# Heads of a two-layer graph network: projections step before the tails in each round

## The chip, the cores and the metric

The kernel runs on one core of one Trainium2 chip. The metric is the device time of one execution in microseconds (us). The engines are TensorE (PE, with its weight loads shown as PEld), VectorE (DVE), ScalarE (ACT), GpSimd (POOL) and SyncE (SP, which issues DMAs here).

## The reference

Two layers, each a graph convolution followed by a feed-forward block, over 3327 nodes of 256 features in fp32. The change touches only the last block, a causal attention with 4 heads and 4 queries per head. Cut to what it computes:

```python
sx = jnp.einsum('bsh,ndh->bnsd', x, hl_w) + hl_b[None, :, None, :]
pad = sx == 0
q = jnp.einsum('bnsd,neod->bneso', sx, wq)
k = jnp.einsum('bnsd,nod->bnso', sx, wk)
v = jnp.einsum('bnsd,nod->bnso', sx, wv)
scores = jnp.einsum('bnesd,bntd->bnest', q, k) * d ** 0.5 + causal
att = jax.nn.softmax(scores, axis=-1)
qkv = jnp.where(pad[:, :, None], 0.0, jnp.einsum('bnest,bntd->bnesd', att, v))
gs = jax.nn.softmax(gate of qkv, axis=-1)
mixed = jnp.einsum('bnsed,bnse->bnsd', ..., gs)
hn = layernorm(mixed + resid, ln_g, ln_b)
hx = relu(fx @ fc1_w.T + fc1_b) @ fc2_w.T + fc2_b     # masked where fx == 0
hx = layernorm(hx + fx, fnorm_g, fnorm_b)
fg = jax.nn.softmax(fout @ fgate_w.T, axis=-1)
return fout * fg (per head)
```

## The kernel before, in words

The nodes are padded to 26 tiles of 128 rows. The two graph layers and the experts come first; the function `heads` runs last, from about 975 us to the end, and is the only one that the change touches.

In `heads`, tile t of queries needs keys and values of tiles 0 to t. A unit is a tile and a head (104 units). The keys of a unit are cut into t // 4 + 1 chunks of at most 512, so there are 392 chunks, and the main loop (line 1422) makes one round for each. A round does, in the order in which the code issues it:

- `drain_to`: the scores of a later chunk are copied from PSUM to SBUF by DVE, with their maxima (`drain`, `sc<-pqk` in the profile). Where none are filled, `fill_next` first issues the matmuls that make them (`fill`, `pqk<-kt,qt`).
- `attend`: the weighted sum of the values on PE (`po<-sc,vr`).
- `turn`: the next chunk's weights are transposed in 32 by 32 blocks by DVE, the stream transposes `sc<-sc`.
- `values`: DMAs for a later chunk, issued by SP (`vr<-vs`).
- `weigh`: exponentials on ACT (`sc<-sc,anmax`), some here and the rest at the round's end.
- `back`: for a unit that ended in the round before, four matmuls with two outputs (`ptO`) and two copies by ACT (`qkv`, `glp`).
- `over`: for a unit that ends in this round, a copy `ot` (by ACT, then a multiply by POOL; for tiles below 5 one multiply by DVE).
- `run(tails)` and `run(preps)`, lines 1438 and 1439: each generator in the list makes one step. These two lines are what the change is about. From tile 8 on they are left out in a round that follows the end of a unit.
- the rest of `weigh`, and `fill_next` if no filled chunk is left.

A prep is the generator `prepare` (line 907), the projections of the next tile. Its nine steps are: a DMA for the row tile (`xres`); mean and variance by DVE (`pst`, `pmv`, `prs`); three POOL operations that make the normalised rows `xn`; their transpose on PE, copied out as `xt`; the projection `psxt` on PE, two ACT copies `sxt`, and the ACT pair Sign and Square into `nz`; four DMAs for `sxd` and the values `pv`, copied to `v`; the keys `pk`, copied to `kt`, and four DMAs that write `vs`; the queries `pq`, copied to `qt`; a transpose back, copied to `sx`. A prep starts in `begin` (line 1376), when the first scores of the tile before are filled. If it isn't finished when its own tile's first scores are due, `begin` runs its remaining steps at once, one after another, without the tails. In tiles 1 to 4 that is most of the prep.

A tail is the generator `tail` (line 1193), the part of a tile after its attention, in 21 steps: a small softmax over the gates (DVE, ACT `gss`, then POOL); POOL's weighted sum into `fx`; a layer norm (`norm4`, line 1169: a DVE sum `l1ns`, four ACT squares `sq`, then seven POOL operations); a transpose copied out as `fxt` and two Sign and Square pairs into `nzf`; the first matmul `ph`, copied out by ACT as `h`; a POOL multiply; the second matmul `ph`, copied out as `fo`, and three POOL operations; a second layer norm (`l2ns`, `sq`, POOL); a transpose copied out as `fot`, and a DMA for `xend`; a gate matmul `pfg`, read by DVE (`fgm`, `fgs`); a softmax; two POOL operations and the store. A tail takes longer than a tile in the early tiles, so up to four or five are in the list there; from about tile 16 one or two.

What sets the order: the class `InOrder` (line 50) chains every instruction of an engine to the one issued before it on that engine. So each engine runs in the order of the program text, and a step that stands second in a round waits behind the first one's instructions on that engine. Semaphores between engines are put in by the framework from the data dependencies and the reuse of buffers.

Buffers that matter: the pool `ps` (line 866) has four PSUM banks under one tag, for everything except `po`: the four score tiles of a chunk, `ptO`, and all outputs of preps and tails. They rotate in the order of the program text, so a new tile waits until the one allocated four before it has been read. The choice between ACT and DVE for a copy out of PSUM is made in `empty` (line 877) from running counters of both engines' work.

## Time and profile before

| what | value |
|---|---|
| time, median of 3 runs (lowest to highest) | 2971.8 us (2970.73 to 2976.79) |
| the profiled execution | 2971.83 us |
| its span, first to last instruction | 2970.1 us |
| mean granted TensorE clock | 0.973 |
| PE busy, 975 us to the end, by stretches of 50 to 200 us | 81 to 96% |
| DVE busy from 2000 to 2900 us | 97% |

The span is the time between the first and the last instruction on the core. Engine names stand first in a row of the profile; `a<-b` reads "a is written from b". A bracket such as `[4.80 <-POOL xn L61]` says that the engine was idle for 4.80 us before the instruction and that POOL's operation on `xn` ended it. All instructions of `heads` carry line 61, the line of the helper that chains them, so tiles, and not lines, tell them apart.

### The profile page before, as it was taken

Reading aid. Unit: us, or ns where it says so; the run is one execution under the profiler, and the core shown is the slowest. Engines: PE = TensorE matmul, PEld = TensorE weight load, DVE = VectorE, ACT = ScalarE, POOL = GpSimd, SP = SyncE. Lnnn points to the kernel's source line nnn. Section 1 sums busy time; section 2 is a strip of 40 time slices with the busy share of each in tenths; the row PEclk is TensorE's granted clock in tenths of the full one; section 3 lists DMA queues with packets and bytes.
Section 4 is the critical chain, followed back from the end, with each engine's and each line's share of the span. In section 5 each row is a group of like instructions: output and inputs, shape, how many; then the busy total and the mean of one; then the engine's idle time right before and its main releaser. Section 6 shows DMA issues by size and latency. Waiting matters only on the chain. (4 is left out here: it accounts for less than half of the span.)

```text
span 2970.1 us, 125328 instructions
## 1 busy us (share of the span) xinstructions
PE 2662.9 (90%) x53422; PEld 1966.3 (66%) x53422; DVE 2398.0 (81%) x5619; ACT 1813.9 (61%) x5128; POOL 973.8 (33%) x1448
## 2 busy tenths in 40 slices
PE   7999988879889788899999999999989999999996
PEld 6878887657668666566666666666666666656664
DVE  5102643689999577789999999999999999999997
ACT  6410135555555457677777776777777677676674
POOL 6441635622231146544433332322222222122121
PEclk9999999999999789999999999999999999999997
DMA  9994568648775222333333443443433433343432
GB/s 377 355 321 135 185 220 276 226 159 285 243 251 169 56 77 77 104 100 106 114 107 104 116 115 106 115 114 112 122 112 113 117 114 114 111 118 110 117 109 77
DMA packets 258188, 449.70 MB, mean 151 GB/s; under 512 B 58816, under 2 KB 156608, under 8 KB 257504
## 3 DMA queue, kind: packets, MB, share of 16 engines
q1 hardware_dynamic: 245536, 417.50, 45.6%
q0 software_dynamic: 6576, 18.02, 1.7%
q8 instruction: 421, 6.90, 1.0%
q10 hardware_dynamic: 5520, 6.18, 0.7%
q14 instruction: 135, 1.11, 0.1%
HBM read 393.37 MB, written 25.88 MB: 141 GB/s over the span
## 5 line engine op out<-in xcount | busy, mean ns | idle before, releaser
L61 ACT ACTIVATE sc<-sc,anmax 128x512 f32<-128x512 f32 (+3 forms) x1568 | 1040.4, 668 | 109.6 <-DVE anmax L61 109.4
L61 PEld LDWEIGHTS po<-sc,vr 32*64 32x64 f32 x43728 | 662.8, 131 | 395.2 <-DVE sc L61 234.0
L61 PE MATMUL po<-sc,vr 32*64 32x128 f32 x43728 | 765.2, 275 | 117.7 <-DVE sc L61 72.3
L61 DVE STREAM_TRANSPOSE sc<-sc 128x2048 f32<-128x2048 f32 (+3 forms) x392 | 816.2, 2082 | 24.2 <-ACT sc L61 23.9
L61 PE MATMUL pqk<-kt,qt 64*128 64x512 f32 (+3 forms) x3136 | 776.2, 579 | 24.5 <-ACT qt L61 4.8
L61 DVE TENSOR_SCALAR_CACHE_REDUCE sc<-pqk 128x512 f32<-128x512 f32 (+2 forms) x1152 | 655.5, 623 | 76.7 <-PE pqk L61 74.7
L61 PEld LDWEIGHTS pqk<-kt,qt 64*128 64x128 f32 x3136 | 319.2, 187 | 247.0 <-issue 102.5
L61 PE MATMUL acc<-wh,p 128*128 128x259 f32 x1352 | 310.0, 387 | 34.5 <-DVE p L61 34.4
L61 PEld LDWEIGHTS acc<-wh,p 128*128 128x128 f32 x1352 | 254.1, 190 | 92.7 <-DVE p L61 52.2
L61 PE MATMUL acc<-y,pan 128*128 128x256 f32 x1352 | 303.5, 385 | 12.2 <-DMA pan<-in_adjt_dram 10.5
L61 POOL TENSOR_TENSOR ot<-ot,sxd 128x512 f32<-128x512 f32 x83 | 105.7, 1273 | 601.1 <-ACT ot L61 588.2
L61 ACT ACTIVATION_READ_ACCUMULATOR sc<-sc,anmax 128x1 f32 x1568 | 299.4, 191 | 0.0
L61 PEld LDWEIGHTS acc<-y,pan 128*128 128x128 f32 x1352 | 257.8, 192 | 53.0 <-issue 17.5
L61 DVE CUSTOM_DVE_ANT_0 sc<-pqk,mask 128x512 f32<-128x512 f32 (+3 forms) x416 | 242.1, 636 | 38.4 <-PE pqk L61 38.0
L61 ACT ACTIVATE u<-u,d 128x512 f32<-128x512 f32 (+1 forms) x182 | 125.2, 688 | 159.4 <-DVE u L61 159.3
L61 DVE SCALAR_TENSOR_TENSOR u<-bc,d 128x512 f32<-128x512 f32 (+1 forms) x182 | 136.4, 750 | 0.1
L61 DVE SCALAR_TENSOR_TENSOR p<-pan,u 128x512 f32<-128x512 f32 (+1 forms) x182 | 126.9, 697 | 10.2 <-PE acc L61 6.1
L61 ACT COPY qkv<-ptO 128x256 f32<-128x256 f32 x104 | 38.5, 370 | 153.3 <-PE ptO L61 153.0
L61 ACT ACTIVATE junk<-ar 128x1664 bf16<-128x1664 f32 x52 | 82.7, 1591 | 65.9 <-DMA ar<-in_adj_dram 64.8
L61 PE MATMUL ptO<-igw,ot 128*128 128x68 f32 x832 | 117.2, 284 | 5.5 <-issue 2.3
L61 PEld LDWEIGHTS ptO<-igw,ot 128*128 128x128 f32 x832 | 102.4, 193 | 24.1 <-issue 17.5
L61 DVE CUSTOM_DVE_ANT_0 sg<-sg,dst 128x1664 bf16<-128x1664 bf16 (+2 forms) x56 | 99.9, 1791 | 1.2 <-ACT dst L61 1.0
(336 smaller groups left out, 2976.6 us busy)
## 6 DMA issues: line engine op xcount, KB each, us to landing
vr<-vs SPq DMA_DIRECT2D x976, 128.0 KB
ar<-in_adj_dram SPq DMA_DIRECT2D x104, 832.0 KB
vr<-vs SPq DMA_DIRECT2D x544, 96.0 KB
pan<-in_adjt_dram SPq DMA_DIRECT2D x156, 256.0 KB
pan<-in_adjt_dram SPq DMA_DIRECT2D x26, 1024.0 KB
pan<-in_adjt_dram SPq DMA_DIRECT2D x20, 832.0 KB
w1e<-w SPq DMA_DIRECT2D x59, 256.0 KB
took<-places SPq DMA_DIRECT2D x59, 129.0 KB
```

The lines of the kernel that those rows point to most:

```text
L61: made = make(*args, **kw)
```

## The change

In each round of the main loop that steps both lists, `run(preps)` is called before `run(tails)`. Nothing else is changed.

```diff
                 if not ended or u["t"] < 8:
+                    run(preps)
                     run(tails)
-                    run(preps)
                 ended = last
```

## The prediction

> **What bounds the kernel now.** First the page's busy line, then the same busy times in stretches, to see where the heads stage (from about 975 us) has room.

> ```profile
> PE 2662.9 (90%) x53422; PEld 1966.3 (66%) x53422; DVE 2398.0 (81%) x5619; ACT 1813.9 (61%) x5128; POOL 973.8 (33%) x1448
> ```
> ```profile
> 1250.00:1300.00 50.00, 45.07 (x1119) 32.13 (x1124) 40.36 (x102) 32.32 (x103) 24.28 (x34) 0.93 0.31 90
> ...
> 2200.00:2400.00 200.00, 184.24 (x5492) 125.98 (x5478) 195.36 (x444) 142.37 (x440) 47.80 (x67) 1.00 0.40 114
> ```

> Columns: stretch, length, busy PE, PEld, DVE, ACT, POOL, clock, DMA. The averages hide two regimes. Late, DVE is busy 195.36 of 200: an order can win only from the last 2 to 3%. At 1250 to 1300 nothing is full (PE 90%, DVE 81%): waits in chains set the pace. So I read PE's waits from 975 to 1500, then the rounds behind the longest.

> ```profile
> PE pt L61 <- POOL xn L61: 20.3, 6, 4.9
> ```
> ```profile
> 1199.88 0.23 POOL L61 TENSOR_SCALAR l2ns<-l2ns 128x4 f32<-128x4 f32 x1
> ...
> 1203.64 0.72 POOL L61 TENSOR_TENSOR fo<-fo,fnb 128x256 f32<-128x256 f32 x1
> ...
> 1204.32 0.56 POOL L61 TENSOR_TENSOR prs<-prs,nhalf 128x1 f32<-128x1 f32 x1
> ...
> 1206.20 0.69 PE L61 MATMUL pt<-ident,xn 128*128 128x128 f32 x2 [4.80 <-POOL xn L61]
> ```
> ```profile
> 1208.50 0.56 DVE L61 TENSOR_SCALAR_CACHE_REDUCE sc<-pqk 128x384 f32<-128x384 f32 x1 [3.01 <-PE pqk L61]
> ```

> This is tile 6. POOL works through a tail's second layer norm (l2ns to fnb); only then come the projection's three operations (prs, xn, xn). PE stands 4.80 us at the transpose of xn with the next scores behind it, and DVE then idles 3.01 us.

> [...] the scores at 1206.82 start after the late transpose. [...] Granted after the wait of 3.85 us in tile 7:

> ```profile
> 1258.00:1265.00 7.00, 7.00 (x127) 4.17 (x127) 4.37 (x9) 4.62 (x14) 0.00 (x0) 0.58 0.01 2
> ```

> Its eight score matmuls took 3.79 us (1258.13 to 1261.92); at 1638 four of the same shape took 1.03, so 2.06 for eight. [...]

> **The change part by part.** No instruction is added or removed. In each round that has both, every engine gets the projection's step before the tails'. Engine choice in `empty` stays: added up along the loop, the counters' margin from tile 2 on, where tails exist, is at least 1.5 towards ACT, and no swapped copy reaches that.

> (a) xn first on POOL, with gains in four rounds (waits 1.92, 4.80, 3.85, 1.41 in tiles 5 to 8; the other two of the six, at 978 and 1002, have no tail beside them). Tile 6: POOL is free at 1199.8 (end of ot), prs and xn need 1.83 (1204.32 to 1206.15), so xn is there at 1201.7 and PE waits 0.5 instead of 4.80. ACT: xt at 1202.8, the tail's fxt and nzf 1.16 (1201.54 to 1202.70), so the exponentials start at 1203.9, not 1207.20: 3.3 earlier; they last 3.9, and PE's values are then done, so ACT's 0.59 idle before ot goes too. DVE finishes the round's softmax at 1205.49 and goes on at once. In the following round the last copy out of PSUM is now h, about 3.85 after ot begins (ot 0.57, sxt 0.72, nz 0.85, fot 0.37, nzf 0.88, h 0.46): 1211.7, with a score pair (0.9) and its reduction (0.69) 1213.3, where 1216.93 was. Gain 3.6. Tile 7 alike: exponentials from 1255.5, ot at 1259.8 (1264.99 before, held by matmuls at the low clock), end at 1265.3 instead of 1270.23. Gain 4.8. In tiles 5 and 8 DVE had work through PE's wait; ACT alone gains. 0.3 each. Sum 9.0. The tail's norm ends 1.8 later, at 1206.2; the transpose that reads it follows no sooner than 1208.6 even with PE early, so the delay has cover of about 2.4; without it, it would cost the 1.8.

> (b) Key copies before the squares. Tiles 13 to 15:

> ```profile
> 1640.18 0.35 ACT L61 ACTIVATE sq<-fo,l2ns 128x64 f32<-128x64 f32 x1
> ...
> 1640.53 0.62 ACT L61 COPY kt<-pk 128x256 f32<-128x256 f32 x2
> ```
> ```profile
> 1640.93 1.13 PE L61 MATMUL pqk<-kt,qt 64*128 64x512 f32 x4 [1.25 <-ACT kt L61]
> ```

> Four squares (1638.76 to 1640.62) stand before kt, whose banks the scores need. PE waits 1.25, 1.24, 1.75; DVE behind it 1.07, 0.69, 0.46. Gain 2.2.

> (c) The gate's bank. A tail's pfg is read by DVE after a 2.3 us transpose; four banks rotate, so its place decides which score waits:

> ```profile
> 1968.66 0.61 PE L61 MATMUL pfg<-fgw,fot 128*128 128x4 f32 x4
> 1969.20 1.16 PE L61 MATMUL pq<-sxt,wq 64*128 64x128 f32 x16
> ...
> 1971.83 1.52 PE L61 MATMUL pqk<-kt,qt 64*128 64x384 f32 x6 [0.82 <-DVE gsm L61]
> ```

> Last in the order, it holds only the last score tile. Beside pq (tiles 17 to 20): 0.75, 0.75, 0.25, 0.25, from DVE's later waits there, up to 0.87; 2.0. Beside psxt (tiles 20 to 23, PE waits 0.72 to 0.75): a half of the stalled pair, 0.46 each, of which 0.45 reach DVE (next waits 0.41 to 0.58); 1.8. Beside pv (tiles 9 to 12, waits 1.00 to 0.34): 0.4 each; 1.6. Sum 5.4.

> (d) The cost: where psxt meets a tail's fot and ph (tiles 5 to 12), nz's two operations come before the copies that free two score banks.

> ```profile
> 1316.94 0.46 ACT L61 ACTIVATE h<-ph,fb 128x256 f32<-128x256 f32 x1
> 1317.30 0.20 ACT L61 ACTIVATE gss<-gss 128x16 f32<-128x16 f32 x1
> 1317.40 0.61 ACT L61 ACTIVATE sxt<-psxt,hlb 128x128 f32<-128x128 f32 x2
> ```

> The last copy moves from sxt to h: later by nz 0.87, earlier by gss 0.20: 0.67. Bounds per round 0 (DVE behind) to 0.67; I take 0.4. Tiles 6 and 7 have it in their sums; six others: 2.4.

> (e) At nothing: SP (xres, sxd, vs move past xend and the store; the store waits on POOL up to 9.7 us, so they can only go earlier, and vr loads keep their place behind both); DVE's pst before a tail's fgs (0.75 later, one bank, DVE busy meanwhile; uncovered, 0.75 in two tiles); the long forced runs of tiles 1 to 4, where DVE waits 7 to 9 us. There `begin` runs the steps one after another with no tail, and in the round before, xt moves ahead of the squares but sxt still follows the same four exponentials on a full ACT (1084 to 1090): 0.2 in all, left out.

> (b) and (c) are terms below 1 us, each of which needs that nothing else ends at the same instant; I keep two thirds of 7.6: 5.1. Sum: 9.0 + 5.1 - 2.4 = 11.7 us gained. The profiled execution took 2971.83 us (span 2970.1 and 1.7 around it) and the median is 2971.8, so one base serves: 2960.

> **Rivals.** The lead is absorbed: something I did not follow ends just behind each removed wait (ACT is full in most rounds of tiles 5 to 8), (a) keeps a third, 3.0, and (b), (c) a third, 2.5, against 2.4: 2969. For it: tiles 5 and 8 show that a PE wait can cost DVE nothing. Against: DVE's idle 3.01 and 3.44 us end on exactly these scores.

> More: the wait's clock penalty and the lead spare further stalls in tiles 6 to 9, (a) doubles: 2951. For it: waits of 3.33 and 2.21 us follow in the same tiles; against: their chains run over DVE.

> Slower: banks held by ACT. If at each meeting of psxt with fot and ph the reductions already wait for the last scores (they do at 1317, 1.03 and 0.18), the full 0.67 falls due in eight tiles, 5.4, and in the rounds with ph and pk kt's 0.63 stands before fo in the same eight, 5.0; with (a) and the rest keeping 4, that is 6.4 lost: 2978. It decides from the point where DVE reaches the third reduction before ACT has ended h's copy.

> **How the numbers follow.** What this measurement can tell from no change is about 0.2%, 5.9 us. Forecast 2960, own range 2953 to 2965.8: 0.58. More, 2951 and below: 0.08. Absorbed, 2966 to 2977: 0.21. Slower, from 2978: 0.13. Faster 0.58 + 0.08 = 0.66, same 0.21, slower 0.13. The range 2951 to 2974 leaves out the slower case and part of the bigger one and of the absorbed one's end, together about 0.2.

> **What would show it.** In the profile after: the waits PE pt on POOL xn fall from 20.3 to near 9; the scores of tile 7 run at a clock near 1; PE's waits on ACT kt vanish at tiles 13 to 15; the pqk waits on DVE's gsm and fgs are shorter and on fewer matmuls; waits on ACT h grow in tiles 5 to 12. It is wrong if DVE's idle time between 1150 and 1320 is not shorter by about 8 us, or if PE now waits for POOL's fo.

## The result and the profile after

The changed kernel takes 2958.7 us (median of 5, 2950.95 to 2960.65) where the one before takes 2971.8 us. The ratio is 0.9954, 95% interval 0.9933 to 0.9975, so 13.7 us are gone (13.1 by the two medians; here and below a gain is what the ratio leaves of the time before). Two later comparisons on other occasions gave 0.9940 (0.9925 to 0.9955) and 0.9969 (0.9957 to 0.9981): 17.9 and 9.2 us. The forecast was 11.7. The profiled execution after has a span of 2958.9 us.

The page's busy line of the changed kernel, engine by engine:

```profile
PE 2658.6 (90%) x53422; PEld 1966.2 (66%) x53422; DVE 2399.3 (81%) x5619; ACT 1810.6 (61%) x5128; POOL 973.1 (33%) x1448
```

Busy times are those of before within 5 us and the counts are the same. So what went was mostly idle time, and the question is where. DVE makes one stream transpose `sc<-sc` in each of the 392 rounds, so the ends of these transposes are a clock of the rounds. By it tiles 5 to 8 lasted from about 1154.0 to 1358.6 before and from 1156.0 to 1349.3 after. Busy times of both stretches (length, then PE, PEld, DVE, ACT, POOL, granted clock, DMA share, GB/s), first of the kernel before:

```profile
1154.00:1358.60 204.60, 182.34 (x4305) 126.70 (x4304) 167.34 (x430) 150.88 (x500) 104.57 (x149) 0.97 0.35 98
```

The same stretch of the changed kernel:

```profile
1156.00:1349.32 193.32, 180.38 (x4308) 125.73 (x4305) 167.42 (x429) 150.93 (x500) 104.65 (x148) 1.00 0.36 105
```

11.3 us less for the same work: DVE, ACT and POOL are equal to 0.1 us, PE takes 2 us less, at a mean granted clock of 1.00 instead of 0.97. DVE's waits in that stretch (total, times, longest), before:

```profile
DVE sc L61 <- PE pqk L61: 28.5, 24, 3.4
```

And after:

```profile
DVE sc L61 <- PE pqk L61: 15.7, 19, 2.4
```

The wait that the forecast started from, among PE's waits between 975 and 1500 us of the changed kernel; it was 20.3:

```profile
PE pt L61 <- POOL xn L61: 8.7, 3, 4.9
```

Of the three that are left two have no tail beside them (at the start of the stage). The third is tile 6. POOL's timeline there, start and duration:

```profile
1199.60 1.28 POOL L61 TENSOR_TENSOR ot<-ot,sxd 128x512 f32<-128x512 f32 x1 [4.20 <-ACT ot L61]
1200.84 0.56 POOL L61 TENSOR_TENSOR prs<-prs,nhalf 128x1 f32<-128x1 f32 x1
1201.36 0.62 POOL L61 TENSOR_TENSOR xn<-xres,pmv 128x256 f32<-128x256 f32 x1
1202.06 0.61 POOL L61 TENSOR_TENSOR xn<-xn,prs 128x256 f32<-128x256 f32 x1
1202.75 0.23 POOL L61 TENSOR_SCALAR l2ns<-l2ns 128x4 f32<-128x4 f32 x1
...
1206.60 0.72 POOL L61 TENSOR_TENSOR fo<-fo,fnb 128x256 f32<-128x256 f32 x1
```

And PE's:

```profile
1202.72 0.44 PE L61 MATMUL pt<-ident,xn 128*128 128x128 f32 x2 [0.46 <-POOL xn L61]
```

The projection's three operations now follow `ot` at once and the tail's norm comes behind them. PE waits 0.46 us where it waited 4.80; forecast was 0.5.

### The profile page after: what moved, and what is told of

Same layout as the page of the kernel before. It is cut to its first block, busy times and chain, and to the rows that moved or that the text cites. A ratio compares the mean times of both kernels' runs of the same rounds, so it can differ in the third digit from the quotient of the medians.

```text
span 2958.9 us, 125328 instructions
## 1 busy us (share of the span) xinstructions
PE 2658.6 (90%) x53422; PEld 1966.2 (66%) x53422; DVE 2399.3 (81%) x5619; ACT 1810.6 (61%) x5128; POOL 973.1 (33%) x1448
## 5 line engine op out<-in xcount | busy, mean ns | idle before, releaser
L61 ACT ACTIVATE sc<-sc,anmax 128x512 f32<-128x512 f32 (+3 forms) x1568 | 1039.8, 668 | 107.8 <-DVE anmax L61 107.6
L61 PEld LDWEIGHTS po<-sc,vr 32*64 32x64 f32 x43728 | 663.6, 131 | 398.9 <-DVE sc L61 230.2
L61 PE MATMUL po<-sc,vr 32*64 32x128 f32 x43728 | 767.6, 276 | 122.2 <-DVE sc L61 72.7
L61 DVE STREAM_TRANSPOSE sc<-sc 128x2048 f32<-128x2048 f32 (+3 forms) x392 | 816.4, 2083 | 25.4 <-ACT sc L61 24.5
L61 PE MATMUL pqk<-kt,qt 64*128 64x512 f32 (+3 forms) x3136 | 776.1, 578 | 20.6 <-ACT qt L61 5.7
L61 DVE TENSOR_SCALAR_CACHE_REDUCE sc<-pqk 128x512 f32<-128x512 f32 (+2 forms) x1152 | 655.1, 623 | 61.5 <-PE pqk L61 60.0
L61 PEld LDWEIGHTS pqk<-kt,qt 64*128 64x128 f32 x3136 | 320.3, 188 | 243.7 <-issue 102.5
L61 PE MATMUL acc<-wh,p 128*128 128x259 f32 x1352 | 309.2, 386 | 35.6 <-DVE p L61 35.4
L61 PEld LDWEIGHTS acc<-wh,p 128*128 128x128 f32 x1352 | 253.7, 190 | 93.2 <-DVE p L61 53.4
L61 PE MATMUL acc<-y,pan 128*128 128x256 f32 x1352 | 301.9, 384 | 12.0 <-DMA pan<-in_adjt_dram 10.3
L61 POOL TENSOR_TENSOR ot<-ot,sxd 128x512 f32<-128x512 f32 x83 | 105.7, 1273 | 589.8 <-ACT ot L61 577.9
L61 ACT ACTIVATION_READ_ACCUMULATOR sc<-sc,anmax 128x1 f32 x1568 | 299.3, 191 | 0.0
L61 PEld LDWEIGHTS acc<-y,pan 128*128 128x128 f32 x1352 | 256.9, 192 | 52.8 <-issue 18.3
L61 DVE CUSTOM_DVE_ANT_0 sc<-pqk,mask 128x512 f32<-128x512 f32 (+3 forms) x416 | 242.2, 637 | 36.9 <-PE pqk L61 36.7
L61 ACT ACTIVATE u<-u,d 128x512 f32<-128x512 f32 (+1 forms) x182 | 125.3, 689 | 159.3 <-DVE u L61 159.2
L61 DVE SCALAR_TENSOR_TENSOR u<-bc,d 128x512 f32<-128x512 f32 (+1 forms) x182 | 136.0, 748 | 0.1
L61 DVE SCALAR_TENSOR_TENSOR p<-pan,u 128x512 f32<-128x512 f32 (+1 forms) x182 | 127.3, 700 | 10.3 <-PE acc L61 6.1
L61 ACT COPY qkv<-ptO 128x256 f32<-128x256 f32 x104 | 38.3, 368 | 150.6 <-PE ptO L61 150.4
L61 ACT ACTIVATE junk<-ar 128x1664 bf16<-128x1664 f32 x52 | 82.7, 1591 | 65.0 <-DMA ar<-in_adj_dram 63.8
L61 PE MATMUL ptO<-igw,ot 128*128 128x68 f32 x832 | 117.2, 285 | 4.3 <-DVE mx L61 2.4
L61 PEld LDWEIGHTS ptO<-igw,ot 128*128 128x128 f32 x832 | 102.3, 194 | 23.6 <-issue 14.6
L61 DVE CUSTOM_DVE_ANT_0 sg<-sg,dst 128x1664 bf16<-128x1664 bf16 (+2 forms) x56 | 99.9, 1791 | 1.2 <-ACT dst L61 1.0
```

Source lines behind the costliest of these rows:

```text
L61: made = make(*args, **kw)
```

## Experiments

Each kernel is compared with the one before, run beside it on the same chip; its profile gives one trace. "Projections first" and "tails first" name the order within a round.

**Which step of the projections carries the gain.** A mark set ahead of each `yield` of `prepare` names the step that is due.

```diff
+                first = due.get("step") == "xn"
+                if first:
+                    run(preps)
                 run(tails)
-                run(preps)
+                if not first:
+                    run(preps)
```

> Projections go first only in the rounds whose projection step is xn on POOL; in all others the tails stay first. Theory POOL queue (the gain is the normalised rows no longer standing behind a tail's layer norm on POOL, tiles 5 to 8): 9 to 11 us less than before, about 2961; the round-by-round lead over before reaches 9 to 11 us at the start of tile 9 and stays there. Rival many small terms (half the gain is bank order, squares and copies over all tiles): 4 to 6 us less, and the lead at tile 9 is under 6. PE's wait pt on POOL xn is near 9 either way.

> The counterpart: projections first in every round except those whose projection step is xn. Theory POOL queue: 0 to 3 us less than before (2969 to 2972), lead at tile 9 within 2 of zero, PE's wait pt on POOL xn stays near 20. Rival many small terms: 5 to 8 us less, about 2965.

With `xn` alone first: 0.9964 (0.9951 to 0.9977), 10.7 us. Only the place of three POOL operations differs in those rounds. In the trace, which is of the slowest of its eight executions, tiles 5 to 8 take 195.5 us where they took 204.5, so 9.0 us were gained there, and from tile 9 to 15 nothing (256.7 and 244.4 us, before 256.3 and 244.6). PE's wait in the first kernel:

```profile
PE pt L61 <- POOL xn L61: 8.5, 3, 4.8
```

With all but `xn` first: 0.9982 (0.9975 to 0.9989), 5.4 us, more than the 0 to 3 that the theory gave to the rest. Tiles 5 to 8 take 205.6 us, none gained, and the wait stands as it was:

```profile
PE pt L61 <- POOL xn L61: 19.3, 6, 5.0
```

So the 9 us of tiles 5 to 8 are POOL's queue. All 14 traces of this document bear it out: with `xn` behind the tail's step (4 traces) these tiles take 201.2 to 205.6 us, with `xn` ahead (10 traces) 189.6 to 198.8. But a single trace can't give the size to a microsecond, as seven traces with one and the same order up to tile 8 spread from 189.6 to 196.5. Something worth about 5 us lies elsewhere. Tiles 13 to 15 of the second kernel point to it: 239.5 us, 5 less than before.

**Where in the run.**

```diff
+                first = u["t"] < 9
```

and `u["t"] >= 9` for the second, with the same branch as above.

> Projections first only while the round's tile is 8 or lower. Theory POOL queue: 9 to 11 us less than before, and the lead from tile 9 to the end stays as it is at tile 9, apart from 1 to 2 us of scatter. Rival many small terms: 4 to 6 us less.

> Projections first only from tile 9 on. Theory POOL queue: 0 to 3 us less than before; at tiles 13 to 15 PE's waits on ACT kt (4.2 us before) are gone, which gives 1.6 to 2; the gate's bank gives less than 1 in the end. Rival many small terms: 5 to 7 us less (the forecast's terms for key copies and the gate's bank, 2.2 and 5.4, in full).

To tile 8: 0.9966 (0.9955 to 0.9978), 10.1 us; tiles 5 to 8 take 189.8. From tile 9: 0.9964 (0.9951 to 0.9976), 10.7 us, far more than either theory gave. Its trace shows only part: 3.3 us of it in tiles 5 to 8, where its order is that of before, and 5.9 us in tiles 13 to 15. The two parts add up to 20.8 us where the whole gave 13.7, 17.9 and 9.2; totals of single kernels carry something that isn't the order. The last experiment shows what that can be.

**The keys, and the two steps together.** The branch with `== "pk"`, and with `in ("xn", "pk")`; and the changed kernel once more.

> The changed kernel once more, for its total and for a second trace. Theory POOL queue plus key copies (about 11 us in tiles 5 to 8, 3 to 5 in tiles 13 to 15, next to nothing elsewhere): 12 to 16 us less than before, and tile by tile the same durations as in the first trace of it, apart from single stalls of PE of 1 to 2 us that no wait explains. Rival scatter (the 5 us of tiles 13 to 15 are such stalls, not the order): 9 to 11 us less, and tiles 13 to 15 together take as long as in the traces with the old order there (243.9 to 244.6 us).

> Projections first only in the rounds with the step that makes the keys, tails first in all others. Theory key copies (the four squares ahead of kt cost DVE its first wait behind PE's and the one of the next round too): tiles 13 to 15 take 3 to 5 us less than in the traces with the old order there (243.9 to 244.6), the rest is unchanged, total 2 to 5 us less than before. Rival as forecast: 2.2 at most, total 0 to 2 less.

> Projections first only in the rounds with xn or the keys. Theory (these two steps carry the gain, bank order and nz cancel): the time of the changed kernel within 3 us, 11 to 16 less than before. Rival, the other steps matter: over 4 us slower than the changed kernel (the gate's bank, 5.4 in the forecast's sum before its two thirds) or over 2 faster (nz).

The changed kernel again: 17.9 us, above the 12 to 16 expected; its tiles 13 to 15 take 241.3 us, so the gain there is no chance, and the rival falls. Over all 14 traces these tiles take 243.9 to 244.6 us with the keys second (3 traces) and 236.1 to 241.3 with the keys first (11). Keys alone: 0.9986 (0.9978 to 0.9993), 4.2 us, tiles 13 to 15 in 237.0, the other groups within 4 us of before either way. Both steps: 0.9956 (0.9942 to 0.9971), 13.1 us. That is 4.8 less than the whole change beside it by the ratios, 3.4 by the medians, where the theory had set 3 and the rival over 4, and the intervals overlap. That the two steps carry most of the gain is shown; whether the others cancel or add some us is not.

Durations by groups of tiles, from one trace of each (us; the order within the group in brackets, K for the keys first, X for xn first, not X for all but xn first):

| kernel | 5 to 8 | 9 to 12 | 13 to 15 | 16 to 20 | 21 to 25 |
|---|---|---|---|---|---|
| before | 204.5 (old) | 256.3 (old) | 244.6 (old) | 489.8 (old) | 592.1 (old) |
| e3, to tile 8 | 189.8 (new) | 257.0 (old) | 243.9 (old) | 495.3 (old) | 593.1 (old) |
| e4, from tile 9 | 201.2 (old) | 257.8 (new) | 238.7 (new) | 493.8 (new) | 591.1 (new) |
| e1, xn only | 195.5 (X) | 256.7 (X) | 244.4 (X) | 498.2 (X) | 593.0 (X) |
| e7, keys only | 201.8 (K) | 257.0 (K) | 237.0 (K) | 493.4 (K) | 593.5 (K) |
| e2, all but xn | 205.6 (not X) | 258.0 (not X) | 239.5 (not X) | 489.5 (not X) | 591.5 (not X) |
| e8, xn and keys | 191.8 (XK) | 257.6 (XK) | 236.1 (XK) | 492.6 (XK) | 594.8 (XK) |
| after, first trace | 193.3 (new) | 256.6 (new) | 239.7 (new) | 493.1 (new) | 593.0 (new) |
| after, second (e5) | 193.4 (new) | 257.2 (new) | 241.3 (new) | 494.7 (new) | 591.8 (new) |
| after, third (e10) | 192.9 (new) | 256.9 (new) | 240.5 (new) | 490.4 (new) | 589.1 (new) |

In each column the mean of the traces marked old (two) less that of those marked new (four): 10.5, -0.5, 4.2, -0.4 and 1.3, together 15.1 us, and the three totals of the changed kernel average 13.6.

**The price of nz.** `nonzero(nz, sxt)` and the four `sxd` DMAs move behind the copy of `v`, into the next step; then the same for the projections of tiles 10 and later only, with the changed kernel beside it.

```diff
-                nz = self.work.tile([P, 2, P], F32, tag="xn", name="nz", bufs=1)
-                nonzero(nz, sxt)
...
-                sxd = self.work.tile([P, 4, P], F32, tag="sxd", name="sxd", bufs=3)
...
                 empty(v, pp, D)
+                nz = self.work.tile([P, 2, P], F32, tag="xn", name="nz", bufs=1)
+                nonzero(nz, sxt)
+                sxd = self.work.tile([P, 4, P], F32, tag="sxd", name="sxd", bufs=3)
...
                 yield
```

> The changed kernel with the projection's Sign and Square into nz, and the four sxd DMAs that read it, moved behind the copy of v in the next step, so that they no longer stand ahead of a tail's copies on ACT. Theory cost (nz ahead of those copies holds score banks in tiles 5 to 12, the forecast's term d of 2.4 us): 1 to 3 us less than the changed kernel, in tiles 5 to 12. Rival no cost left (the lead from xn covers it): within 1 us of the changed kernel, tiles 9 to 12 within 0.5.

For all tiles: 0.9944 (0.9927 to 0.9961), no better than the changed kernel (0.9940), where 1 to 3 us less was expected. Tiles 9 to 12 gain 0.4 to 1.0 us (256.2), but tile 5 takes 47.3 us, where the changed kernel's three traces have 43.5, 43.5 and 45.1. There nz now stands on ACT just ahead of the squares, six exponentials and the copies of the keys. PE's timeline in tile 5:

```profile
1182.11 2.26 PE L61 MATMUL pqk<-kt,qt 64*128 64x384 f32 x5 [1.77 <-ACT kt L61]
```

In the first trace of the changed kernel this wait on the keys is 1.02 us. Here the stretch from 1175 to 1200 us ran at a granted clock of 0.86, and the same work of the changed kernel (1172 to 1195) at 1.00.

> The changed kernel with nz and its DMAs moved behind the copy of v for the projections of tiles 10 and later only (rounds of tile 9 on), so that the keys of tile 5 don't wait for it. Theory cost (nz ahead of the copies holds score banks in tiles 9 to 12): 1 to 3 us less than the changed kernel in the same call; tiles 9 to 12 together 1 us or more below the 256.6 and 257.2 us of the changed kernel's two traces, tile 5 near 43.5. Rival given back: within 1 us of the changed kernel.

From tile 9 on only: 2953.1 us (median of 6), 0.9939 (0.9924 to 0.9955), beside the changed kernel's 2960.2 and 0.9969. It beats both kernels by the medians, and its interval lies below that of the changed kernel. Tiles 9 to 12 take 254.8 us, 2.1 less than the mean of the three traces of the changed kernel. Tile 5, expected near 43.5 us, took 45.2, and tiles 5 to 8 took 196.0, 2.6 more than in any of those three traces, though the order there is the same. What happens behind them is plain in tile 9. ACT in the changed kernel:

```profile
1362.13 0.42 ACT L61 ACTIVATE nz<-sxt 128x256 f32<-128x256 f32 x1
1362.58 0.42 ACT L61 ACTIVATE nz<-nz 128x256 f32<-128x256 f32 x1
1362.90 0.35 ACT L61 COPY fot<-pt 128x256 f32<-128x256 f32 x1
```

PE behind it:

```profile
1361.99 1.03 PE L61 MATMUL pqk<-kt,qt 64*128 64x384 f32 x4
1363.31 1.41 PE L61 MATMUL pqk<-kt,qt 64*128 64x384 f32 x4 [0.30 <-ACT fot L61]
```

PE in the kernel with nz moved:

```profile
1362.47 2.42 PE L61 MATMUL pqk<-kt,qt 64*128 64x384 f32 x8
```

The third score tile needs the bank that `fot` empties. With nz out of the way the eight matmuls run through. The traces account for 2 of the 7 us between the two medians; the rest isn't explained by the order.

**The stalls that no wait explains.** PE also stands for up to 2.2 us in the middle of its work, with "issue" as the cause: no semaphore that the profile shows ended the wait. In tile 7 the first trace of the changed kernel has this; PE's timeline:

```profile
1246.29 1.93 PE L61 MATMUL po<-sc,vr 32*64 32x128 f32 x114 [0.66 <-ACT ot L61]
1249.69 0.47 PE L61 MATMUL po<-sc,vr 32*64 32x128 f32 x14 [1.47 <-issue]
1250.09 1.11 PE L61 MATMUL ptO<-igw,ot 128*128 128x68 f32 x8
1251.03 0.39 PE L61 MATMUL pt<-ident,xn 128*128 128x128 f32 x2
1251.26 0.38 PE L61 MATMUL pt<-ident,fx 128*128 128x128 f32 x2
```

> The changed kernel beside the previous one on the same chip: 13 to 18 us less than before if the order's effects read off the traces round by round (about 15) are all there is; tile 7 again with the stall of 1.47 us inside the weighted sum (114 of 128 matmuls done) if that stall belongs to the place in PE's order, without it if it is chance.

The third trace has it again: 1.47 us after 114 of 128. It is no chance. Its total, 9.2 us less than before (5.6 to 12.8), is below what was expected.

```diff
-            def turned(src, dst):
+            def turned(src, dst, extra=0):
...
+                for _ in range(extra):
+                    nc.tensor.transpose(pt[:, 0, :], src[:, :P], self.ident)
```

> The changed kernel with 60 more transposes of the first half of xn ahead of tile 0's two, which write the same bank and are overwritten; every later matmul stands 60 places further back in PE's instruction stream. Theory instruction supply (PE stands where a new block of about 127 matmuls with their weight loads has to arrive): the stalls move 60 matmuls forward in the work; in tile 7 the one of 1.47 us stands after 54 of the 128 matmuls of the weighted sum, not after 114, and all stalls keep their count from the start of the stream (7753, 8516, 8643, 13913). Rival (the stall belongs to the place in the work, a bank or a transfer): after 114 of 128 again. The time grows by about 60 times the 0.19 us of a transpose at most, 11 us.

> The same with 128 more transposes, about one whole block. Theory instruction supply: the stalls stand where they did in the work, within 2 matmuls: in tile 7 after 113 to 115 of 128. Rival (any added work moves them, or chance): elsewhere or gone. The time grows by at most 128 times 0.19 us, 24 us.

With 128 more, PE in tile 7:

```profile
1268.79 1.93 PE L61 MATMUL po<-sc,vr 32*64 32x128 f32 x114 [0.37 <-issue]
1272.46 0.47 PE L61 MATMUL po<-sc,vr 32*64 32x128 f32 x14 [1.75 <-issue]
```

With 60 more:

```profile
1250.66 2.08 PE L61 MATMUL po<-sc,vr 32*64 32x128 f32 x128 [1.52 <-ACT ot L61]
```

After a whole block the stall is back at 114 of 128. After 60 it is gone from there. It doesn't stand at 54 of 128 either, where it was expected. That half of the expectation failed. But of the 37 stalls behind 1100 us in this trace, 36 lie within 3 matmuls of the spacing found in the changed kernel's three traces, carried on from the start of the stream (such as 19697, 19824 and 19952), and none within 3 of that spacing moved along with the work. The one left, at 13973, is 13913 plus 60, with 1.15 us in every trace: a place in the work. The times of the two, 2969.8 and 2986.1 us beside 2973.7 for the kernel before, come from one execution each, too few to read a cost from.

That these stalls are waits for instructions can be read from the traces. Instructions arrive by a DMA queue that the page counts (transfers, MB, share of 16 engines' time), for the changed kernel:

```profile
q8 instruction: 421, 6.90, 1.0%
```

That is 16 KB a transfer. PE ran 107,982 instructions in this trace (matmuls, weight loads, and the semaphore and register instructions of its sequencer), 421.8 times 256, so these are PE's; the two kernels with more transposes have 422 transfers. The 14 traces together, from 975 us on, hold 523 stalls of PE with "issue" as the cause. Of these, 496 stand at the 194th or 195th instruction of a block of 256, counted from PE's first, in the kernels with more transposes too. In each of the 496 exactly as many transfers have landed as whole blocks lie behind, and the stall ends 1.15 to 1.65 us after the last landing; by chance such a stretch would catch a tenth of them, since transfers come about 5 us apart. The other 27 stand at three places of the work, one of them the 13913 above.

The landings also tell why the boundary in tile 7 passes unseen with 60 more transposes. Its transfer landed at 1247.57 us, PE was then held by `ot` for 1.52 us, and the weighted sum began at 1250.66 with the instructions there. In the first trace of the changed kernel it landed at 1248.32, when 114 of the 128 matmuls were done.

## Why the prediction held, step by step

**(a) xn first on POOL: right in kind, 9.0 forecast.** The gain in tiles 5 to 8 is 10.5 us, and 9.0 in the kernel that moved nothing else. By rounds, each named by the chunk whose weights it transposes: tile 6, round (head 1, chunk 0), 9.15 and 9.18 us with the old order, 5.85 in all three traces of the changed kernel; tile 7, round (1, 0), 10.42 and 10.45, then 7.13 (8.1 and 8.3 in the kernel with nz moved from tile 9 on and in the one with 128 more transposes, which have that order too). By tiles, as means of the table's old and new traces, tile 6 gave 5.0 (forecast 3.6), tile 7 gave 3.6 (forecast 4.8), and tiles 5 and 8 gave 0.4 and 1.5, where 0.3 each was put, since only ACT was thought to gain there. That the sum came near 9.0 is in part luck, as one tile fell short and others gave more. The sign set for it came: DVE's waits on scores fell by 12.8 us in tiles 5 to 8, where about 8 was asked for. In tile 7 PE no longer waits for `xn`, and the granted clock over its scores is 1.00, as said (the eight take 2.15 us; before, behind the wait of 3.85 us, they took 3.79 at a granted clock of 0.50 from 1258 to 1262),

```profile
1250.00:1254.00 4.00, 4.00 (x57) 2.85 (x52) 3.50 (x9) 2.73 (x9) 3.21 (x5) 1.00 0.56 168
```

but the stall of 1.47 us shown above stands ahead of the transpose. In e3 and in the kernel with 60 more transposes, which lack it, the next round takes 4.92 us, where it takes 6.89 in the changed kernel; these 2.0 us are more than the difference to 4.8. With the old order such a stall costs nothing there. The kernel with keys alone has it, and its wait on `xn` is shorter than the 3.85 of before by more than the stall lasts:

```profile
1259.65 0.47 PE L61 MATMUL po<-sc,vr 32*64 32x128 f32 x13 [2.02 <-issue]
...
1262.93 0.69 PE L61 MATMUL pt<-ident,xn 128*128 128x128 f32 x2 [1.55 <-POOL xn L61]
```

Its round takes 10.46 us all the same. The tail's later norm had its cover: PE waits for POOL's `fo` only in the last tile, as before.

**(b) Keys before the squares: mis-sized, the term that failed.** The forecast was 2.2 us, cut to two thirds with (c). Comparing the kernel with keys alone with traces that have the keys second, in rounds that hold no stall, gives 1.0, 1.0 and 1.6 us in tiles 13 to 15, 3.6 in all. The waits of PE on `kt` are gone there. Most of the gain of tile 15 was overlooked, because only DVE's first wait behind PE's, 0.46 of the 1.6 us, was counted. PE in tile 15 before:

```profile
1797.13 1.27 PE L61 MATMUL pqk<-kt,qt 64*128 64x512 f32 x4 [1.75 <-ACT kt L61]
```

And DVE:

```profile
1798.29 0.69 DVE L61 TENSOR_SCALAR_CACHE_REDUCE sc<-pqk 128x512 f32<-128x512 f32 x1 [0.46 <-PE pqk L61]
...
1802.55 0.69 DVE L61 TENSOR_SCALAR_CACHE_REDUCE sc<-pqk 128x512 f32<-128x512 f32 x1 [0.73 <-PE pqk L61]
```

PE stays late, so the next round's scores are late too: 0.46 and 0.73, and then a little more. In the changed kernel the keys come first on ACT:

```profile
1783.76 0.64 ACT L61 COPY kt<-pk 128x256 f32<-128x256 f32 x2
1784.29 0.36 ACT L61 ACTIVATE sq<-fo,l2ns 128x64 f32<-128x64 f32 x1
```

and PE's eight matmuls run through, with no wait of DVE in this round and the next:

```profile
1783.06 2.52 PE L61 MATMUL pqk<-kt,qt 64*128 64x512 f32 x8
```

**(c) The gate's bank: 5.4 forecast, about 3 found.** By their places in the rounds: beside `pq` 0.6 us in tile 17 (0.75 forecast), nothing sure in tiles 18 to 20, where rounds move both ways (in tile 19 one gains 1.5 to 2.2 us and two others lose 1.5 and 0.6); beside `psxt` exactly 0.45 at the first round of tiles 21, 22 and 24, but in tiles 21 and 22 the next round gives 0.44 and 0.45 back; beside `pv` 1.7 in tiles 9 to 12 (1.6 forecast). No kernel changed this term alone, so its parts are read from places, not shown. The wait of the scores on `gsm` fell from 4.1 to 0.9 us behind 1110 us; the one on `fgs`, which was to fall too, rose from 3.4 to 4.6.

**(d) The cost of nz: right.** 1.6 us were put for tiles 9 to 12. New against old order costs 1.7 in the rounds behind `psxt` there, and moving nz away wins 2.1. The place named was wrong by one copy: PE waits for `fot` (0.30 us in tile 9), not for `h`, whose waits did not grow.

**Rivals.** "Absorbed" and "slower" fell: DVE's idle time went with PE's waits, and the keys ahead of `fo` cost 0.2 us a tile at tiles 9, 10 and 12, not the 0.63 that "slower" needed. "More" asked for 20.7 us; the three gains lie below that, though the interval of the second reaches 22.3. With measured terms the sum is 10.5 + 3.6 + 3 - 1.7 - 0.5 (the last for the keys ahead of `fo`), or 15. The forecast of 11.7 was low by (b), 3.6 against 1.5 after its cut to two thirds, and by tiles 5 to 8, 10.5 against 8.2 with the cost of nz in tiles 5 and 8 taken off; the second is within the spread of the traces. The 13.7 of the first comparison has both 11.7 and 15 in its interval (7.4 to 19.9).

## What to carry to other kernels

When two streams of steps are chained into one order on each engine, look first at the engine that no busy share points to: a three-operation step of 1.8 us behind a seven-operation norm on POOL set the pace of PE and DVE (4.80 and 3.01 us idle in tile 6). Price a removed wait by following the late engine until it has caught up, not by the next engine's first wait. And compare kernels round by round in several traces before explaining a few us of their totals.

## What the runs showed of the hardware

PE's instruction supply shows in its idle time. Total, number and longest of PE's unexplained stalls in the weighted sum, from 975 us on, in the kernel before:

```profile
PE po L61 <- issue: 23.6, 25, 1.8
```

In the changed kernel, first trace:

```profile
PE po L61 <- issue: 31.2, 35, 2.0
```

In its second trace they are 33.5, in its third 26.9 us. Those at the block boundaries, whatever the matmul, come to 25.9 us before and 31.8, 33.3 and 28.0 in the changed kernel's traces. So PE stands at these boundaries for about 1% of this run; how much of it the run would get back is not shown, since a stall can replace another wait (with keys alone, 2.02 us of stall and then 1.55 on `xn`, where the wait was 3.85). In none of the 14 traces did PE pass a boundary sooner than 1.18 us after the landing of its transfer, and a transfer took 0.88 to 2.46 us. Whether a stall is seen then depends on how far PE was held up before: in tile 7 a wait of 1.51 us on `ot` just ahead of the weighted sum goes with no stall, in the trace of before and in that of e3 (1.52), and a shorter wait (0.66) with one of 1.47. That PE, once freed of waits, runs into its own supply more often fits these numbers, but e4, with the old order up to tile 8, has 31.5 us of such stalls too; it was not tested alone, and neither was how much of the scatter of totals comes from it.
